# Value projection's first passes and their scaling placed ahead of the third chunk's u, and block 1's norm and transposes behind them

## The chip, the cores and the metric

The kernel runs on one NeuronCore of a Trainium2 chip. TensorE (PE) multiplies, VectorE (DVE), ScalarE (ACT) and GpSimd (POOL) do elementwise work, and SyncE (SP) issues most DMA transfers. The metric is the device time of one execution in microseconds; lower is better.

## The reference

The input is 8192 tokens (4 sequences of 2048) of 256 features, float32. One layer is computed, attention in chunks of 32 tokens and then a gated feed-forward network, each with a residual and a layer norm after it:

```python
Q, K, V = x @ W_q.T, x @ W_k.T, x @ W_v.T
mask[i, j] = decay ** (i - j) if i >= j else 0        # 32 x 32, decay = sigmoid(log_decay[0])
S = (Q K^T within each chunk) * mask
O = S V within each chunk
attn = (sigmoid(x @ W_g.T) * O) @ W_o.T + x
h = layernorm(x + attn)
u = silu(h @ wg.T) * (h @ wu.T)                       # 768 hidden features, int weights / 127
out = layernorm(h + u @ wd.T)
```

## The kernel before

**Tiling.** The tokens are cut into NB = 16 blocks of 512. Features lie on the 128 partitions where a matmul contracts over them (KD = 2 halves of 256), and tokens lie on the partitions where a norm runs over the features. The 768 hidden features are six chunks of 128, numbered hc = 0 to 5. PSUM has eight banks of 128 x 512 float32, one pool of which every product takes one in turn.

**Split products.** To keep float32 accuracy, a projection of the attention is three products. `token_parts` (L471 and on) splits the tokens x into x_hi (ScalarE, L479), x_lo (GpSimd, L480) and x_gap (VectorE, L486); the weights are split likewise. `three` (L533 and on) multiplies hi with hi and lo with lo into two PSUM banks (the first passes), has ScalarE scale each bank in place (L540), and returns a function that later adds the third product, gap with gap (the gap passes), and finishes. TensorE's gap passes need the scaled bank. `split_v` does so for the values v of a block (tile p_v, matmuls L521; its end, the v copies, on ScalarE at L572); `split_y`, `split_gate` and `split_out` do it for p_y, p_g (both L499) and p_o (L521).

**The feed-forward's chunks.** `ffn_up` (L822 and on) makes one hidden chunk: eight matmuls (L833) into the banks fg and fu; s = silu(fg) on ScalarE (L842); then, in its inner function `multiply`, u = fu * s on VectorE (L853), its cast u_hi on ScalarE (L858) and the remainder u_lo on GpSimd (L859). With `held=True` it returns `multiply` instead of calling it, so that other work can be put between s and u. `up_now` is `ffn_up` for one chunk, without holding. `ffn_down` (fdn, L704) contracts the six chunks' u_hi and u_lo.

**Norm and transposes.** `normalize` (L433) is four ScalarE instructions, one for each 128 tokens. `move_h` takes the normed h of a block: four 32 x 32 block transposes on VectorE into sq (L785), then 16 DMA transfers from SP into hT (L792). `split_h` casts hT to hT_hi on ScalarE (L809), and GpSimd makes hT_lo (L810); the next block's chunks multiply these.

**The loop.** Three blocks are in work at once. In pass b of the main loop (b = 0 to 13), the feed-forward of block b, the attention of block n = b + 2, the projections of block m = b + 3 and the loading of xT for block m + 1 are interleaved; m exists (`more`) for b = 0 to 12. Below, "block b" means pass b of this loop. Before block 0 stand the weights' preparation and the first blocks' attention; after block 13 the last two feed-forwards are finished.

**What sets the order.** Each engine works through its own queue. The order in it is the order in which the source lists the instructions, since most of them are recorded with `in_turn` or `in_steady_turn`, which fix it by hand; transfers from SP and some of GpSimd's work are placed by a scheduler. So the order of the calls in the loop is the order on TensorE, ScalarE and VectorE. The part of pass b that the change touches reads, before:

```python
        if b == 0:
            normalize(hs[b + 1], *scales_h)
            moving = move_h(b + 1, hs[b + 1])
        if m + 1 < NB:
            xTs[m + 1] = load_xT(m + 1)
        up_now(b, hT, uT, 2)
        if more:
            v_next, v_rest = split_v(m, x_parts)
            up_now(b, hT, uT, 3)
            v_rest()
```

In block 0 the norm of h_1 stands here, behind chunk 1; in every later block the norm of h_(b+1) stands ahead of chunk 0 and `move_h` behind chunk 1.

Of the kernel before, what the change touches and what calls it, by code (L numbers as in the profile page):

```python
# [76 lines left out]
def kernel(  # L77
# [20 lines left out]
    NB = NT // TB  # L98
# [29 lines left out]
    def load_xT(b, start=None, pieces=1):  # L128
        xt = xin.tile([P, KD, TB], F32, tag="xT", name=f"xT_{b}")
        src = xT[:, span(b, start)].rearrange("(k p) t -> p k t", p=P)  # L130
        n = KD // pieces
        for k in range(0, KD, n):
            queue(start).dma_start(xt[:, k : k + n, :], src[:, k : k + n, :])
        return xt
# [19 lines left out]
    xTs, xns = {}, {}  # L154
# [412 lines left out]
    def split_v(b, x_parts):  # L567
        v = work.tile([P, NG, D], F32, tag="v", name=f"v_{b}")
        per = TB // D

        def finish(i, pb):
            in_turn(nc.scalar.copy(flat(v, slice(i * per, (i + 1) * per)), pb))  # L572

        return v, three(f"v_{b}", token_major(w_parts["wv"], x_parts), finish)
# [68 lines left out]
    def attn_scores(b, yT):  # L643
        xt = xTs.pop(b)
        halves = [slice(i * PAIR, (i + 1) * PAIR) for i in range(P // PAIR)]
        ps = bank(f"ps_{b}")[:, : NG * PAIR].rearrange("p (g c) -> p g c", c=PAIR)
        for g in range(NG):
            for fc in range(KD):
                for rows in halves:
                    tokens = slice(g * P + rows.start, g * P + rows.stop)  # L650
                    product = nc.tensor.matmul(  # L651
                        ps[rows, g, :],
                        lhsT=xt[:, fc, tokens],
                        rhs=yT[:, fc, tokens],
                        start=(fc == 0),
                        stop=(fc == KD - 1),
                    )
                    in_turn(product)
        sTs.append(sTs.pop(0))
        sT = sTs[-1]  # L660
        for rows in halves:
            in_steady_turn(
                nc.vector.tensor_tensor(sT[rows, :, rows], ps[rows], mask[rows], ALU.mult)  # L663
            )
        return sT.rearrange("p g c -> p (g c)")
# [156 lines left out]
    def ffn_up(b, hT, uT, chunks, cols=slice(0, TB), held=False):  # L822

        n = cols.stop - cols.start
        for hc in chunks:
            pg = bank(f"fg_{b}_{hc}_{cols.start}")[:, :n]
            pu = bank(f"fu_{b}_{hc}_{cols.start}")[:, :n]

            kinds = (0, 1) if hc % 2 == 0 else (1, 0)
            for kind in kinds:  # L830
                for pb, w in ((pg, fg), (pu, fu)):
                    for dc in range(KD):
                        product = nc.tensor.matmul(  # L833
                            pb,
                            lhsT=w[kind][:, dc, hc * P : (hc + 1) * P],
                            rhs=hT[kind][:, dc, cols],
                            start=(kind == kinds[0] and dc == 0),
                            stop=(kind == kinds[1] and dc == KD - 1),
                        )
                        in_turn(product)  # L840
            s = work.tile([P, n], F32, tag="s", name=f"s_{b}_{hc}")
            in_turn(nc.scalar.activation(s, pg, AF.Silu, scale=SCALE / H_UP))  # L842
            no_more_splits()
            if len(uT[0]) == hc:
                for kind, dtype, tiles in zip(("hi", "lo"), (F32R, F16), uT):
                    tiles.append(
                        acts.tile([P, TB], dtype, tag=f"u_{kind}", name=f"u_{kind}_{b}_{hc}")
                    )

            def multiply(hc=hc, pu=pu, s=s):  # L850
                u = work.tile([P, n], F32, tag="u", name=f"u_{b}_{hc}")
                in_steady_turn(
                    nc.vector.scalar_tensor_tensor(u, pu, U_UP / H_UP, s, ALU.mult, ALU.mult)  # L853
                )
                hi, lo = uT[0][hc][:, cols], uT[1][hc][:, cols]

                def split():
                    in_steady_turn(nc.scalar.copy(hi, u))  # L858
                    nc.gpsimd.tensor_tensor(lo, u, hi.bitcast(F32), ALU.subtract)  # L859

                if lagging:
                    late_splits.append(split)
                else:
                    split()

            if held:
                return multiply
            multiply()
# [167 lines left out]
    def up_now(b, hT, uT, hc):  # L1036
        ffn_up(b, hT, uT, range(hc, hc + 1))

    for b in range(NB - 2):
        n = b + 2  # L1040
        m = b + 3
        more = m < NB
        xns[n] = load_xn(n)
        hT = hTs.pop(b)
        uT = [], []
        yT, v, sg = ahead
        if b:
            normalize(hs[b + 1], *scales_h)
        up_now(b, hT, uT, 0)
        if not more:  # L1050
            sT = attn_scores(n, yT)
        up_now(b, hT, uT, 1)
        if b:
            moving = move_h(b + 1, hs[b + 1])
        if more:
            sT = attn_scores(n, yT)
        if b == 0:
            normalize(hs[b + 1], *scales_h)
            moving = move_h(b + 1, hs[b + 1])
        if m + 1 < NB:  # L1060
            xTs[m + 1] = load_xT(m + 1)
        up_now(b, hT, uT, 2)
        if more:
            v_next, v_rest = split_v(m, x_parts)
            up_now(b, hT, uT, 3)
            v_rest()
            if scales_out is not None:
                normalize(r_before, *scales_out)
                store(b - 2, r_before)
        goT = attn_values(n, sT, v, sg)  # L1070
        if b == 0:
            look_up(range(4, n_pieces))
            cast_fd(0)
        if b == 1:
            count = count_wide()
            n_wide_early = const.tile([1, 1], I32, tag="n_wide_early", name="n_wide_early")
            nc.vector.tensor_copy(n_wide_early, count)
        go_parts, go_gaps = token_parts(goT, f"go_{n}")
        if more:
            y_next, y_rest = split_y(m, x_parts)  # L1080
        else:
            up_now(b, hT, uT, 3)
            normalize(r_before, *scales_out)
            store(b - 2, r_before)
        up_now(b, hT, uT, 4)
        go_gaps()
        up_now(b, hT, uT, 5)
        if b == 0:
            cast_fd(1)
        elif more:  # L1090
            hTs[b + 1] = split_h(b + 1, moving)
        r_before = r_out
        if more:
            y_rest()
            sg_next, g_rest = split_gate(m, x_parts)
            hs[n], out_rest = split_out(n, go_parts)
            g_rest()
            mv_h = out_rest()
            if b == 0:
                hTs[b + 1] = split_h(b + 1, moving)  # L1100
            ahead = y_next, v_next, sg_next
            if m + 1 < NB:
                x_parts, x_gaps = token_parts(xTs[m + 1], f"x_{m + 1}")
            std_h = root_in_turn(mv_h, of_h, f"h_{b}")
            if b:
                mv_before, std_before = mv_out, root_in_turn(mv_out, of_out, f"out_{b}")
            back_to_silu()

            def between():
                scales = scale_and_shift(mv_h, std_h, of_h, f"h_{b}")  # L1110
                if m + 1 < NB:
                    x_gaps()
                return scales

            r_out, mv_out, scales_h = ffn_down(b, uT, hs.pop(b), between)
            if b:
                scales_out = scale_and_shift(mv_before, std_before, of_out, f"out_{b}")
        else:
            hs[n], out_rest = split_out(n, go_parts)
            hTs[b + 1] = split_h(b + 1, moving)  # L1120
            scales_out = iterated_scale_and_shift(mv_out, of_out, f"out_{b}")
            normalize(r_before, *scales_out)
            store(b - 1, r_before)

            def amid():
                return iterated_scale_and_shift(out_rest(), (HALF, 1.0), f"h_{n}")

            r_out, mv_out, scales_h = ffn_down(
                b, uT, hs.pop(b), chunkwise=True, amid=amid
            )  # L1130
            normalize(hs[n], *scales_h)
            scales_out = iterated_scale_and_shift(mv_out, of_out, f"out_{b + 1}")
# [344 lines left out]
```

## Time and profile before

| | |
|---|---|
| median of 3 runs | 514.29 us (513.94 to 514.57) |
| the profiled execution's own time | 515.19 us |
| its span, first to last instruction | 513.6 us |
| TensorE matmul busy | 503.7 us, 98% of the span |
| ScalarE / VectorE / GpSimd busy | 73% / 60% / 57% |
| mean granted TensorE clock | 0.999 of full speed |

All times below are microseconds from the start of the span, unless they are durations. A row of the timeline has its start, its busy time, the engine, the source line, the operation with output <- inputs, and after an x how many like instructions it holds; in brackets may stand the idle time of the engine ahead of it and what ended that. A list of waits names the waiting engine and work, what it waited for, and then microseconds in total, the number of waits and the longest. PEld is TensorE's loading of weights, which overlaps matmuls.

### The profile page before, as it was taken

Reading aid. Unit: us, or ns where it says so; the run is one execution under the profiler, and the core shown is the slowest. Engines: PE = TensorE matmul, PEld = TensorE weight load, DVE = VectorE, ACT = ScalarE, POOL = GpSimd, SP = SyncE. Lnnn points to the kernel's source line nnn. Section 1 sums busy time; section 2 is a strip of 40 time slices with the busy share of each in tenths; the row PEclk is TensorE's granted clock in tenths of the full one; section 3 lists DMA queues with packets and bytes.
Section 4 is the critical chain, followed back from the end, with each engine's and each line's share of the span. In section 5 each row is a group of like instructions: output and inputs, shape, how many; then the busy total and the mean of one; then the engine's idle time right before and its main releaser. Section 6 shows DMA issues by size and latency. Waiting matters only on the chain.

```text
span 513.6 us, 9691 instructions
## 1 busy us (share of the span) xinstructions
PE 503.7 (98%) x3480; PEld 399.4 (78%) x3480; DVE 309.3 (60%) x725; ACT 373.1 (73%) x701; POOL 292.2 (57%) x324
## 2 busy tenths in 40 slices
PE   9999899999999999999999999999999999999995
PEld 5788677788878879787787878778787787877684
DVE  3977667564564647547474564647547464665654
ACT  4868686676868777686786868777686786766845
POOL 2835546554746557465464846557465564657764
PEclk9999999999999999999999999999999999999999
DMA  7720312112222122222212222122222211103112
GB/s 243 235 84 20 94 25 82 42 43 68 73 74 74 43 78 88 60 64 83 83 43 71 84 61 75 45 77 86 61 64 82 83 44 30 54 14 98 35 36 69
DMA packets 43315, 36.83 MB, mean 72 GB/s; under 512 B 4865, under 2 KB 39169, under 8 KB 43265
## 3 DMA queue, kind: packets, MB, share of 16 engines
q1 hardware_dynamic: 42144, 35.28, 22.9%
q10 hardware_dynamic: 1120, 0.92, 0.6%
q8 instruction: 28, 0.46, 0.4%
q14 instruction: 23, 0.18, 0.1%
HBM read 20.45 MB, written 8.39 MB: 56 GB/s over the span
## 4 chain that ended last, share of the span: by engine, by line
PE 74%; DVE 8%; ACT 7%; SPq 4%; issue 3%; POOL 2%; DMA 1%; DVEq 0%; ACTq 0%; POOLq 0%
PE fg L833 13%; PE fu L833 12%; PE fdn L704 11%; PE p_y L499 7%; PE p_g L499 7%; PE p_v L521 6%; PE p_o L521 6%; PE po L673 5%; SPq L792 4%; DVE u L853 3%; PE ps L651 2%; ACT s L842 2%; ACT h L433 1%; PE fdn L907 1%; DMA out_dram<-r 1%
## 5 line engine op out<-in xcount | busy, mean ns | idle before, releaser
L859 POOL TENSOR_TENSOR u_lo<-u,u_hi 128x512 f16<-128x512 f32 (+1 forms) x98 | 128.7, 1315 | 100.9 <-ACT u_hi L858 100.9
L853 DVE SCALAR_TENSOR_TENSOR u<-fu,s 128x512 f32<-128x512 f32 (+1 forms) x98 | 66.6, 680 | 127.1 <-ACT s L842 103.7
L858 ACT CAST u_hi<-u 128x512 fp32r<-128x512 f32 (+1 forms) x98 | 59.9, 612 | 85.0 <-DVE u L853 84.9
L833 PE MATMUL fg<-hT_hi,fg_hi 128*128 128x512 f32 (+1 forms) x196 | 71.1, 444 | 0.0
L842 ACT ACTIVATE s<-fg 128x512 f32<-128x512 f32 (+1 forms) x98 | 56.8, 580 | 6.3 <-PE fg L833 6.2
L833 PE MATMUL fu<-hT_hi,fu_hi 128*128 128x512 f32 (+1 forms) x196 | 60.6, 390 | 0.0
L833 PE MATMUL fg<-hT_lo,fg_lo 128*128 128x512 f16 (+1 forms) x196 | 58.2, 378 | 0.0
L833 PE MATMUL fu<-hT_lo,fu_lo 128*128 128x512 f16 (+1 forms) x196 | 57.4, 375 | 0.0
L480 POOL TENSOR_TENSOR go_lo<-goT,go_hi 128x512 fp32r<-128x512 f32 x30 | 38.7, 1313 | 26.3 <-ACT go_hi L479 26.3
L480 POOL TENSOR_TENSOR x_lo<-xT,x_hi 128x512 fp32r<-128x512 f32 x30 | 38.3, 1298 | 24.2 <-ACT x_hi L479 18.0
L744 DVE TENSOR_TENSOR h<-p_o,x 128x512 f32<-128x512 f32 x30 | 19.3, 686 | 42.5 <-PE p_o L521 32.4
L704 PE MATMUL fdn<-fd_hi,u_hi 128*128 128x256 f32 x312 | 44.7, 285 | 0.0
L833 PEld LDWEIGHTS fu<-hT_hi,fu_hi 128*128 128x128 f32 x196 | 36.5, 188 | 8.5
L833 PEld LDWEIGHTS fg<-hT_hi,fg_hi 128*128 128x128 f32 x196 | 34.7, 189 | 9.5
L704 PEld LDWEIGHTS fdn<-fd_hi,u_hi 128*128 128x128 f32 x312 | 39.0, 188 | 0.3
L433 ACT ACTIVATE h<-h,shift_h,scale_h 128x256 f32<-128x256 f32 x52 | 27.0, 590 | 16.8 <-POOL shift_h L396 16.8
L704 PE MATMUL fdn<-fd_lo,u_lo 128*128 128x256 f16 x312 | 38.6, 273 | 0.0
L810 POOL TENSOR_TENSOR hT_lo<-hT,hT_hi 128x512 f16<-128x512 f32 x28 | 35.5, 1290 | 3.7 <-ACT hT_hi L809 3.7
L833 PEld LDWEIGHTS <-fu_lo 128*128 128x128 f16 x196 | 19.2, 98 | 22.4 <-issue 0.3
L673 PE MATMUL po<-sT,v 128*128 128x128 f32 x256 | 31.2, 275 | 0.3 <-DVE sT L663 0.3
L704 PEld LDWEIGHTS <-u_lo 128*128 128x128 f16 x312 | 28.4, 98 | 3.9
L673 PEld LDWEIGHTS po<-sT,v 128*128 128x128 f32 x256 | 30.0, 192 | 0.7 <-PE p_v L521 0.5
(176 smaller groups left out, 1067.2 us busy)
## 6 DMA issues: line engine op xcount, KB each, us to landing
x<-in_x_dram SPq DMA_DIRECT2D x16, 512.0 KB, 3.5
xT<-in_xT_dram SPq DMA_DIRECT2D x15, 512.0 KB, 3.7
hT<-sq SPq DMA_DIRECT2D x224, 32.0 KB, 1.9
out_dram<-r SPq DMA_DIRECT2D x13, 512.0 KB, 3.1
out_dram<-r SPq DMA_DIRECT2D x7, 128.0 KB, 1.7
fg_int<-in_ffn_gT_dram SPq DMA_DIRECT2D x3, 256.0 KB, 7.0
fu_int<-in_ffn_uT_dram SPq DMA_DIRECT2D x3, 256.0 KB, 7.2
fd_int<-in_ffn_dT_dram SPq DMA_DIRECT2D x3, 256.0 KB, 5.9
```

The costliest lines, as they stand in the source:

```text
L433: nc.scalar.activation(r[:, g, :], r[:, g, :], AF.Identity, bias=shift[:, g : g + 1], scale=scale[:, g : g + 1],)
L480: in_turn(nc.gpsimd.tensor_tensor(lo[:, k, :], t[:, k, :], whole, ALU.subtract))
L499: nc.tensor.matmul(pb, lhsT=a[kind][:, k, i * P : (i + 1) * P], rhs=b[kind][:, k, :], start=kind + k == 0, stop=True, skip_group_check=True,)
L521: nc.tensor.matmul(pb[:, j * D : (j + 1) * D], lhsT=b[kind][:, k, g * P : (g + 1) * P], rhs=a[kind][:, k, :], start=kind + k + j == 0, sto ...
L673: product = nc.tensor.matmul(po[:, cols], lhsT=v[:, g, dc * P : (dc + 1) * P], rhs=sT[:, cols], start=True, stop=True,)
L704: product = nc.tensor.matmul(pb[:, j * D : (j + 1) * D], lhsT=part[:, g * P : (g + 1) * P], rhs=w, start=(i == 0), stop=(i == len(terms) - 1),
L810: nc.gpsimd.tensor_tensor(in_order[1], whole, in_order[0].bitcast(F32), ALU.subtract)
L833: product = nc.tensor.matmul(pb, lhsT=w[kind][:, dc, hc * P : (hc + 1) * P], rhs=hT[kind][:, dc, cols], start=(kind == kinds[0] and dc == ...
L842: in_turn(nc.scalar.activation(s, pg, AF.Silu, scale=SCALE / H_UP))
L853: nc.vector.scalar_tensor_tensor(u, pu, U_UP / H_UP, s, ALU.mult, ALU.mult)
L858: in_steady_turn(nc.scalar.copy(hi, u))
L859: nc.gpsimd.tensor_tensor(lo, u, hi.bitcast(F32), ALU.subtract)
```

## The change

The third chunk (hc = 2) is called with `held=True`, so its matmuls and s are issued, but not yet u. Then `split_v` issues the value projection's first passes and their two scalings, and only then `multiply` issues u, u_hi and u_lo of that chunk. In block 0 the norm of h_1 and `move_h` come after this instead of before the chunk. In block 13 there is no value projection, so the chunk is as it was. No instruction is added or taken out.

In the built program, TensorE's order is the same as before, and so is that of SP's transfers. On ScalarE, blocks 0 to 12 have s_2, p_v scaling, p_v scaling, u_hi_2, s_3 where they had s_2, u_hi_2, p_v scaling, p_v scaling, s_3; in block 0 the four norm instructions stand between u_hi_2 and s_3, where they stood ahead of s_2. On VectorE only block 0 differs: u_2 stands ahead of the four transposes instead of behind them. GpSimd's order is unchanged.

```diff
         if more:
             sT = attn_scores(n, yT)
+        if m + 1 < NB:
+            xTs[m + 1] = load_xT(m + 1)
+        multiply = ffn_up(b, hT, uT, range(2, 3), held=True)
+        if more:
+            v_next, v_rest = split_v(m, x_parts)
+        multiply()
         if b == 0:
             normalize(hs[b + 1], *scales_h)
             moving = move_h(b + 1, hs[b + 1])
-        if m + 1 < NB:
-            xTs[m + 1] = load_xT(m + 1)
-        up_now(b, hT, uT, 2)
         if more:
-            v_next, v_rest = split_v(m, x_parts)
             up_now(b, hT, uT, 3)
             v_rest()
             if scales_out is not None:
```

## The prediction

> **What bounds the kernel.** I read the page first: engine shares, then waits.
>
> ```profile
> PE 503.7 (98%) x3480; PEld 399.4 (78%) x3480; DVE 309.3 (60%) x725; ACT 373.1 (73%) x701; POOL 292.2 (57%) x324
> ```
>
> TensorE is the bound, so only its idle moments can be won or lost. The list of waits over the whole span has one large entry of TensorE on another engine:
>
> ```profile
> PEld p_v L521 <- ACT p_v L540: 6.4, 13, 2.0
> ...
> PE p_v L521 <- ACT p_v L540: 2.5, 3, 1.6
> ```
>
> 13 times, once in each of blocks b = 0 to 12, the gap passes of the value projection (wv_gap times x_gap) wait for ScalarE's scaling of p_v. The timeline shows why; block 0, rows of other work left out:
>
> ```profile
> 56.27 2.08 ACT L433 ACTIVATE h<-h,term_h,y_h 128x256 f32<-128x256 f32 x4
> ...
> 56.73 0.63 PE L521 MATMUL p_v<-wv_lo,x_lo 128*128 128x256 f32 x4
> ...
> 58.26 0.57 ACT L842 ACTIVATE s<-fg 128x512 f32<-128x512 f32 x1
> ...
> 58.55 0.63 PE L833 MATMUL fu<-hT_hi,fu_hi 128*128 128x512 f32 x2
> ...
> 59.64 0.62 ACT L858 CAST u_hi<-u 128x512 fp32r<-128x512 f32 x1 [0.81 <-DVE u L853]
> 60.16 1.06 ACT L540 ACTIVATE p_v<-p_v 128x512 f32<-128x512 f32 x2
> ...
> 60.80 1.22 PE L521 MATMUL p_v<-wv_gap,x_gap 128*128 128x256 f32 x8 [1.61 <-ACT p_v L540]
> 61.15 0.59 ACT L842 ACTIVATE s<-fg 128x512 f32<-128x512 f32 x1
> ```
>
> The first passes end at 57.36 (56.73 + 0.63), yet their scaling starts at 60.16: it stands in ScalarE's queue behind the norm of h_1, s_2, and the cast u_hi_2, which waits 0.81 for u_2. A later block has no norm there, but the same queue:
>
> ```profile
> 182.31 0.63 PE L521 MATMUL p_v<-wv_lo,x_lo 128*128 128x256 f32 x4
> ...
> 183.44 0.62 ACT L858 CAST u_hi<-u 128x512 fp32r<-128x512 f32 x1 [1.68 <-DVE u L853]
> ...
> 183.96 1.06 ACT L540 ACTIVATE p_v<-p_v 128x512 f32<-128x512 f32 x2
> ...
> 184.13 0.63 PE L833 MATMUL fu<-hT_hi,fu_hi 128*128 128x512 f32 x2
> ...
> 184.59 1.02 PEld L521 LDWEIGHTS p_v<-wv_gap,x_gap 128*128 128x128 f32 x8 [0.27 <-ACT p_v L540]
> 184.60 1.21 PE L521 MATMUL p_v<-wv_gap,x_gap 128*128 128x256 f32 x8
> ```
>
> Here the first gap pass is on time, but the row takes 1.21 where p_o's like takes 1.10: the second bank's scaling, done at 185.02, comes late.
>
> I measure each stall by starts. Rows of two 128x512 matmuls follow each other every 0.47 us; eight unstalled 128x256 gap passes take 0.94 (the chain's p_o pieces). So the stall is the start of the next matmul (po), less the start of the last fu row, less 0.47 and 0.94. Block 0: 61.85 - 58.55 - 1.41 = **1.89**. Block 1: **0.94**. Blocks 2 to 12: 0.08, 0.07, 0.11, 0.11, 0.10, 0.10, 0.08, 0.46, 0.08, 0.20, 0.11, together **1.50**. All: 4.33 us.
>
> **What the Trainium skill says.** "TensorE: Matmul & The Clock Gate", section "Architectural detail: the array is 16× 32×32, not 1× 128×128", says that ScalarE and VectorE work strictly first in, first out, while TensorE may only pull weight loads ahead. The trace agrees: ready scaling waits 2.8 us (57.36 to 60.16) behind a cast. "Perfetto Trace Analysis", section "Summary: the profiler window per engine type", says that waits lie outside an instruction's window and that TensorE's end is an estimate; so I use starts, and the trace's p_v rows (0.63 long, 0.47 apart) show the need. "DMA: Bandwidth & Descriptors", section "Anatomy of one DMA — SWDGE (gpsimd) path", gives about 2.0 us fixed per DMA, for GpSimd's path; the hT pieces here, from SP, show 1.8 / 1.9 / 3.6 (min, median, max).
>
> **The change, part by part.** No instruction is added or removed, and the built order of TensorE and of SP's transfers is the same. What moves:
>
> *Blocks 1 to 12, ScalarE.* Two scalings go ahead of u_hi_2. In block 4: s_2 ends 181.75; the first bank's passes end about 181.9, its scaling runs to 182.5; the second's end at 182.94 (182.31 + 0.63), scaling 183.0 to 183.6, over a second before TensorE asks at 184.60. u_hi_2 waited for u_2 until 183.44 anyway (VectorE's order is unchanged here), and now runs 183.55 to 184.15: 0.1 late. Behind it: POOL's u_lo_2 (0.1 late, needed only by u_4's buffer and by fdn, microseconds later) and s_3. s_3 stood behind the scalings at 184.95; now it waits only for its matmuls (183.48 + 0.82 = 184.30): ScalarE gains 0.6 up to the v copies. So each stall goes entirely: block 1's 0.94 and the 1.50. What is late next? The scaling of p_g: in block 3 it frees the bank about 0.2 before TensorE needs it. The 0.6 lead widens that. hT's cast, just ahead of it in ScalarE's queue, could start 0.6 earlier; in block 7 at 287.4 instead of 288.01, the last hT piece having been issued at 284.2 and landing 1.9 later, 286.1. Cost 0; if that cover failed, up to 0.1 a block would return.
>
> *Block 0, ScalarE.* The norm (four, 2.08) goes behind u_hi_2. By rows: s_2 56.27; scalings 56.80 and 57.40 (the second waits for TensorE's 57.36); u_2 on VectorE from 56.95; u_hi_2 57.9; norm 58.42; s_3 60.41 instead of 61.15. That is **0.74** earlier: the 0.81 wait for u_2 is filled. TensorE's stall of 1.89 goes, but ScalarE, 0.74 ahead, is what it meets next. From s_3 to p_o's scaling ScalarE runs without waiting for TensorE (the casts fd_hi and fd_lo are in there), and ends here:
>
> ```profile
> 73.06 1.06 ACT L540 ACTIVATE p_g<-p_g 128x512 f32<-128x512 f32 x2
> ...
> 73.78 1.13 PE L499 MATMUL p_g<-x_gap,wg_gap 128*128 128x512 f32 x4
> 74.05 1.05 ACT L540 ACTIVATE p_o<-p_o 128x512 f32<-128x512 f32 x2
> ```
>
> TensorE would arrive at 73.78 - 1.89 = 71.89; the first p_g bank is scaled at 72.88. It waits there, then for p_o's scalings, and leaves the block 0.74 earlier, not 1.89.
>
> *Block 0, VectorE and SP.* u_2 goes ahead of the four transposes, which follow the norm and end at about 60.98 instead of 58.83, just before s_3 ends and u_3 starts (61.0). hT_1's 16 DMAs (10.3 us of issue) start 2.15 later, and the last lands near 70.7 + 1.9 = 72.6 (74.3 with the longest landing). The cast hT_hi would run at 75.96 - 0.74 = 75.2. So nothing waits. SP's next transfer, x_4, starts at 76.82 when its buffer is free; xT_4 stays ahead of hT_1. PSUM banks: p1_y takes u_2's, fg_4 s_3's, fu_4 u_3's; these are done at 57.7, 61.0 and 61.8 and asked for at about 62.7, 63.6 and 64.1. POOL's u_lo_2 comes earlier.
>
> Sum: 0.74 + 0.94 + 1.50 = **3.18 us** on the profiled execution, 515.19 (span 513.6 and 1.59 around it): 512.0. It is 0.90 above the median of 514.29; of the stalls, block 9's 0.36 above its like and block 11's 0.10 look like chance of this execution. For the median I count 2.8: **511.5 us**.
>
> Costs the trace cannot show: whether VectorE and POOL disturb each other more when their overlaps shift. The nearest row is x_gap in block 0, 2.17 for two against 1.26 in block 1, which I read as one such clash at 0.9; off TensorE's path it costs nothing. I take 0, and -0.3 to +0.9. Block 6 lost about 0.3 at p_g, p_o; a 0.6 lead might save it: 0, bound -0.3.
>
> **Rivals.**
> - *Block 0 keeps all of its 1.89* (p_g not bound by ScalarE): 2.8 + 1.15 gives 510.3. For: other blocks' p_g has some cover. Against: the rows above, with ScalarE 0.2 from TensorE already.
> - *The wait moves on in every block* to p_g or p_o, and only part is won: blocks 0 and 1 alone give 1.68, 512.6; block 0 alone gives 513.55, within noise. For: ScalarE is busy 73% and its margin at p_g was 0.2. Against: the 0.6 it gains.
> - *Slower: hT_1 lands too late.* Place: ScalarE's queue ahead of x_hi, and POOL's chain to shift_h, on which block 1's norm already waited 1.8. Each microsecond past 75.2 delays block 1; about 1.0 is absorbed at block 1's p_v. To end 1.03 slower it must lose 2.8 + 1.03, so land after about 80; that needs a mean issue near 1.1 us instead of 0.6. One issue of 1.69 is the longest seen; were all like it, landing at 61 + 27 + 1.9 = 90 would cost some 13: 525. Against: the median issue is 0.595.
> - *Nothing changes*, because scheduling restores the old order: the built order excludes it.
>
> **How the numbers follow.** About 0.2%, 1.03 us, is what a measurement of this kernel can tell from no change. Forecast as worked: 0.70. All of block 0: 0.08. Only part: 0.15, of which 0.05 within 1.03. Slower: 0.05, and 0.02 for a small loss within it. So faster 0.88, same 0.07, slower 0.05. The range runs from 510.4 (3.18 with block 6's 0.3 and a little of block 0's rest) to 513.0 (block 1's or the later stalls half kept, a clash of 0.9 on the path).
>
> **What would show it.** In the trace after: the wait of p_v on the p_v scaling nearly gone (6.4 to under 1); eight p_v gap passes 0.94 before po in every block; in block 0, ScalarE in the order s_2, p_v, p_v, u_hi_2, norm, s_3 at 60.4, and a new stall of about 1 at p_g there; period of later blocks about 30.55 instead of 30.6 to 31.0. It is wrong if p_g or p_o gap passes of later blocks wait more than 0.1, if hT_hi waits for DMA, or if block 0 gains clearly other than 0.74.

## The result, and the profile after

The changed kernel takes a median of **510.81 us** (510.29 to 511.66, 4 runs) against 514.29 (513.94 to 514.57, 4 runs): ratio 0.9934, 95% interval 0.9917 to 0.9951. The gain is 3.48 us; the forecast was 511.5 (510.4 to 513.0), so the result lies inside the range, 0.7 below the time forecast. The profiled execution took 511.11, span 509.6, at a mean granted clock of 0.998. From the page of the changed kernel:

```profile
PE 501.2 (98%) x3480; PEld 400.3 (79%) x3480; DVE 309.3 (61%) x725; ACT 375.6 (74%) x701; POOL 291.8 (57%) x324
```

TensorE's busy time fell by 2.5 us with as many instructions, part of it in the gap rows of p_v, which take 1.10 where they took 1.21. Its waits on the other engines, in the two lists of waits (TensorE's matmuls, its weight loads):

```profile
PE p_g L499 <- ACT p_g L540: 0.9, 1, 0.9
...
PEld p_g L499 <- ACT p_g L540: 1.2, 2, 1.1
...
PEld p_o L521 <- ACT p_o L540: 0.2, 1, 0.2
```

The 13 waits of p_v on its scaling (6.4 us) are gone from both; one new stall stands at p_g. Block 0 in the timeline after (this execution reached block 0 0.56 sooner, so 0.56 is to be added when a start is compared with one before):

```profile
55.70 0.59 ACT L842 ACTIVATE s<-fg 128x512 f32<-128x512 f32 x1
...
56.19 1.23 ACT L540 ACTIVATE p_v<-p_v 128x512 f32<-128x512 f32 x2
...
57.33 0.61 ACT L858 CAST u_hi<-u 128x512 fp32r<-128x512 f32 x1
...
57.84 2.08 ACT L433 ACTIVATE h<-h,term_h,y_h 128x256 f32<-128x256 f32 x4
57.99 0.63 PE L833 MATMUL fu<-hT_hi,fu_hi 128*128 128x512 f32 x2
...
58.46 1.10 PE L521 MATMUL p_v<-wv_gap,x_gap 128*128 128x256 f32 x8
...
59.40 1.95 PE L673 MATMUL po<-sT,v 128*128 128x128 f32 x16
59.82 0.58 ACT L842 ACTIVATE s<-fg 128x512 f32<-128x512 f32 x1
...
71.73 1.05 ACT L540 ACTIVATE p_g<-p_g 128x512 f32<-128x512 f32 x2
72.36 0.30 PEld L499 LDWEIGHTS p_g<-x_gap,wg_gap 128*128 128x128 f32 x2 [1.06 <-ACT p_g L540]
72.36 1.21 PE L499 MATMUL p_g<-x_gap,wg_gap 128*128 128x512 f32 x4 [0.86 <-ACT p_g L540]
```

ScalarE runs s_2, two scalings, u_hi_2, norm, s_3 with no wait between, but for 0.13 within the row of scalings, where the second bank's first passes end. From the last fu row to po are 59.40 - 57.99 = 1.41 us, exactly a row of two (0.47) and eight gap passes (0.94): no stall at p_v. The 1.89 has become a stall at p_g and p_o. Block 4, answering to the rows shown before:

```profile
179.61 0.58 ACT L540 ACTIVATE p_v<-p_v 128x512 f32<-128x512 f32 x1 [0.28 <-PE p_v L521]
...
180.55 0.58 ACT L540 ACTIVATE p_v<-p_v 128x512 f32<-128x512 f32 x1 [0.36 <-PE p_v L521]
...
181.04 0.61 ACT L858 CAST u_hi<-u 128x512 fp32r<-128x512 f32 x1
...
181.70 0.63 PE L833 MATMUL fu<-hT_hi,fu_hi 128*128 128x512 f32 x2
...
181.96 0.60 ACT L842 ACTIVATE s<-fg 128x512 f32<-128x512 f32 x1 [0.30 <-PE fg L833]
182.17 1.10 PE L521 MATMUL p_v<-wv_gap,x_gap 128*128 128x256 f32 x8
...
183.11 1.05 PE L673 MATMUL po<-sT,v 128*128 128x128 f32 x8
```

ScalarE's waits are now on TensorE (0.28, 0.36, 0.30): it has caught up. In place of the 1.68 that it stood on u_2 it does the two scalings.

Where the time came from, by TensorE's starts (a block's period is from its first ps matmul to the next block's):

| us | before | after | gained |
|---|---|---|---|
| start of block 0 | 52.33 | 51.77 | 0.56 |
| block 0 | 32.54 | 31.74 | 0.80 |
| block 1 | 31.81 | 30.86 | 0.95 |
| blocks 2 to 12 | 336.08 | 334.29 | 1.79 |
| from block 13 to the end | 60.89 | 60.90 | -0.02 |
| span | 513.65 | 509.56 | 4.08 |

The first row isn't the change's: over all profiled executions here, whatever the kernel, block 0 starts between 50.97 and 52.41. So below I compare the **loop**, block 0 to 12: 400.43 before, 396.89 after, **3.54** less.

### The profile page after: what moved, and what is told of

Read it like the earlier page. It is cut to its first block, busy times and chain, and to the rows that moved or that the text cites. A ratio compares the mean times of both kernels' runs of the same rounds, so it can differ in the third digit from the quotient of the medians.

```text
span 509.6 us, 9690 instructions
## 1 busy us (share of the span) xinstructions
PE 501.2 (98%) x3480; PEld 400.3 (79%) x3480; DVE 309.3 (61%) x725; ACT 375.6 (74%) x701; POOL 291.8 (57%) x324
## 4 chain that ended last, share of the span: by engine, by line
PE 90%; DVE 4%; ACT 4%; issue 1%; POOL 1%; DVEq 0%; POOLq 0%; ACTq 0%
PE fg L833 16%; PE fu L833 15%; PE fdn L704 14%; PE p_v L521 8%; PE p_g L499 8%; PE p_y L499 8%; PE p_o L521 7%; PE po L673 5%; PE ps L651 3%; DVE u L853 1%; PE fdn L907 1%; ACT s L842 1%; PE pi L193 1%; PE pg L583 1%; PE pv L625 1%
## 5 line engine op out<-in xcount | busy, mean ns | idle before, releaser
L682 DVE SCALAR_TENSOR_TENSOR goT<-sg,po 128x512 f32<-128x512 f32 x32 | 21.9, 687 | 15.4 <-PE po L673 15.2
```

## The experiments

**The two halves of the change.** Changed kernel, the new order of calls only where a condition holds:

```diff
+        ahead_of_u = b == 0        # block0_only;  b > 0 in later_only
...
         multiply = ffn_up(b, hT, uT, range(2, 3), held=True)
+        if not ahead_of_u:
+            multiply()
         if more:
             v_next, v_rest = split_v(m, x_parts)
-        multiply()
+        if ahead_of_u:
+            multiply()
...
```

(with block 0's norm and transposes where the order needs them). The changed kernel itself ran beside them.

> The changed kernel unaltered, as the yardstick for the other kernels on this chip. My theory: TensorE's stall ahead of p_v's gap passes is gone in blocks 1 to 12 (2.7 us), block 0 is 0.8 shorter, sum 3.5 off the time before: about 510.8. Rival (some of the first difference was chance at the start of the span, which was 0.56 shorter in the changed kernel's profile): 511.3.

> Only block 0 has the new order (scalings ahead of u_hi_2, norm and transposes behind it); blocks 1 to 12 have the old one. My theory: block 0 gains what ScalarE gains, 0.8, and no more, since p_g's scaling is late there; blocks 1 to 12 stall as before (block 1: 0.94, the others 0.07 to 0.46). 0.8 off the time before, 513.5. Rival A, that block 0's move alone frees the later blocks too (an earlier block 0 leaves ScalarE ahead): 510.8. Rival B, that block 0 keeps its whole 1.89: 512.4.

> Only blocks 1 to 12 have the new order; block 0 has the old one. My theory: block 0 stalls 1.89 as before, all other p_v stalls are gone, period of blocks 2 to 12 is 30.55: 2.7 off the time before, 511.6. Rival, that the later blocks' gain rests on block 0's: close to the time before, 513.5 or more.

Measured, against 514.45 before on that chip: changed kernel 511.21 (ratio 0.9931, 0.9917 to 0.9944), block 0 alone 513.46 (0.9984, 0.9977 to 0.9992), later blocks alone 512.17 (0.9951, 0.9938 to 0.9965). The gains add: 0.99 + 2.28 = 3.27 against 3.24. The later half's 2.28 is short of the 2.7 expected, and the changed kernel is nearer to 511.3 than to 510.8; both hold the stretch ahead of block 0, which differs by up to 1.4 from one execution to another. By the loop alone the later half gains 2.74, and the changed kernel's loop takes 396.89 again. The rivals of the two halves are refuted. Within block 0, the move of the scalings and that of the norm were not tried apart. In the traces block 0's period is 31.74 with its own half and 32.54 without. With the later half all blocks from 2 to 11 take 30.55 or 30.56. With block 0's half alone they are as before, and block 6 takes 30.96 and block 9 31.01: to 0.01 us what they took in the trace before.

**Are those larger stalls chance?** The prediction had left 0.46 us out of the sum as "chance of this execution". The kernel before, once more:

> The kernel before, unchanged, for another profiled execution. If the larger stalls of blocks 6 (0.41 longer period), 9 (0.46) and 11 (0.2) were chance of one execution, as the prediction took them, they are elsewhere or absent now: periods of blocks 2 to 12 then all within 30.60 to 30.70. If they belong to the place in the program, the same blocks have them again: block 6 about 30.96, block 9 about 31.01, block 11 about 30.75, and behind them VectorE's u_4 of block 6 and second residual of block 8 about 0.33 late again.

One run, 513.93. Periods of blocks 6, 9, 11: 31.04, 31.02, 30.76 (in the first trace 30.96, 31.01, 30.76). So they are no chance. In each trace of this order VectorE starts u_4 of block 6 about 0.35 late against the other blocks, and the residual r behind the feed-forward (L887, "second residual" in the expectations; the first of its two instructions in the block) of block 8 some 0.3 late (0.24 in the first trace). u_4 in the trace of this run, by VectorE's timeline:

```profile
252.88 0.69 DVE L853 SCALAR_TENSOR_TENSOR u<-fu,s 128x512 f32<-128x512 f32 x1 [4.54 <-PE fg L833]
```

In the changed kernel both delays are still there (u_4 of block 6 at 251.00, 0.35 behind the other blocks'), and no period shows them.

**Do they belong to what those blocks do, or to where they stand in VectorE's instructions?** The kernel before with three, and with twenty, instructions at its start that write an unused tile:

```diff
     nc.vector.memset(eps, EPS)
+    pad = const.tile([P, 1], F32, tag="pad", name="pad")
+    for _ in range(3):             # 20 in pad20
+        nc.vector.memset(pad, 0.0)
```

> The kernel before with three further VectorE instructions at the very start (a 128x1 tile set to 0 three times, well before the first block; nothing reads it). No engine's order is otherwise changed. Theory (the recurring delays of about 0.35 us belong to positions in VectorE's stream of instructions, so three more instructions ahead move them onto others, as in the kernel with fd_lo on VectorE, which has three more too and shows none in blocks 6 and 8): the delays at u_4 of block 6 and at the second residual of block 8 are gone, and with them the extra 0.4 us of the periods of blocks 6 and 9, unless they now stand where they cost as much: up to 0.8 us faster than before, 513.6. Rival (they belong to what those blocks do, or to the time in the execution): still there, periods 30.96 and 31.01, time as before, 514.4.

> The same with twenty such instructions at the start. Theory (position in the stream): the delays stand some twenty VectorE instructions earlier in the work than before, so near the residuals and norm statistics at the end of block 5 and near yT in block 8, or are hidden there; blocks 6 and 9 lose their extra 0.4 unless they are hit again: between 513.6 and 514.4. Rival (place in the work or time): as before, periods 30.96 and 31.01.

With three: 513.84 against 514.47 (0.9985, 0.9977 to 0.9994). Blocks 6 and 9 take 30.62 and 30.63. u_4 of block 6 is on time, and u_1 of block 11 is late instead (lines are three higher in this kernel):

```profile
253.30 0.69 DVE L856 SCALAR_TENSOR_TENSOR u<-fu,s 128x512 f32<-128x512 f32 x1 [4.19 <-ACT s L845]
...
394.15 0.69 DVE L856 SCALAR_TENSOR_TENSOR u<-fu,s 128x512 f32<-128x512 f32 x1 [1.59 <-ACT s L845]
```

The idle time of 1.59 ahead of that u_1 is 1.24 without the three, and block 11 takes 30.98 instead of 30.76. With twenty: 514.19 (0.9997, 0.9988 to 1.0005), blocks 6 and 9 normal, blocks 8 and 11 at 30.93 and 31.00: the delays stand at u_4 of block 8 and at r of block 10. The theory holds: the delays follow the position in VectorE's stream. My guess of where twenty would put them was wrong but for the gain's bounds.

**How much room does ScalarE have now?** The changed kernel with one or two ScalarE instructions more in each of blocks 1 to 12:

```diff
             up_now(b, hT, uT, 3)
             v_rest()
+            if b:
+                for i in range(1):             # 2 in filler2
+                    part = flat(v_next, slice(2 * i, 2 * i + 2))
+                    in_turn(nc.scalar.mul(part, part, 1.0))
```

> The changed kernel with one further ScalarE instruction in each of blocks 1 to 12: half of v multiplied by 1.0 in place behind the v copies, so no value changes; about 0.53 us each, 6.4 us of ScalarE in all. Theory (the change gave ScalarE a lead of about 0.73 us at the p_g bank, and only the lead's end costs time): 0.73 - 0.53 leaves 0.2, so ten blocks keep their 30.55 and only blocks 6 and 9, whose recurring delay is 0.35, stall by about 0.15 each: 0.3 us over the changed kernel, about 511.5. Rival (any ScalarE work in the loop costs its time, the lead is not there): 6.4 us, about 517.5. Rival (the recurring delays were chance): no block stalls, 511.2.

> The changed kernel with two such instructions in each of blocks 1 to 12 (the other half of v too, by 1.0, no value changes): 1.06 us a block. Theory: 0.73 - 1.06 is -0.33, so each of the twelve blocks stalls about 0.33 at the p_g and p_o gap passes, or slightly less where another wait further on gives it back: up to 4.0 us, with 0.35 more in blocks 6 and 9: about 515.5. Rival (ScalarE is no limit at p_g): 511.2, no stall. Rival (all ScalarE work costs): 12.7 us, about 524.

Against 514.76 on that chip: 511.80 (0.9946, 0.9932 to 0.9959) and 518.53 (1.0078, 1.0063 to 1.0094). In the loop, one costs 0.85 over the changed kernel and two cost 6.43 (0.3 and 4.3 expected). So the lead is real, but I had it too large. Block 4, ScalarE's scaling of p_o and TensorE's gap passes on it, in the kernel before:

```profile
197.73 1.04 ACT L540 ACTIVATE p_o<-p_o 128x512 f32<-128x512 f32 x2
...
198.54 1.10 PE L521 MATMUL p_o<-wo_gap,go_gap 128*128 128x256 f32 x8
```

in the changed kernel:

```profile
194.76 1.08 ACT L540 ACTIVATE p_o<-p_o 128x512 f32<-128x512 f32 x2
...
195.98 1.10 PE L521 MATMUL p_o<-wo_gap,go_gap 128*128 128x256 f32 x8
```

and with one filler:

```profile
195.05 1.05 ACT L540 ACTIVATE p_o<-p_o 128x512 f32<-128x512 f32 x2
...
195.66 1.02 PEld L521 LDWEIGHTS p_o<-wo_gap,go_gap 128*128 128x128 f32 x8 [0.17 <-ACT p_o L540]
195.77 1.11 PE L521 MATMUL p_o<-wo_gap,go_gap 128*128 128x256 f32 x8
```

From the scaling's start to the gap passes are 0.81, 1.22 and 0.72; at 0.72 the weight load waits and the period is 0.04 longer. So p_o runs short before the 0.73 that I had put at p_g is used: measured from there, the lead at p_o is 0.50 at most, and before the change it was 0.09. One filler of 0.53 uses it up: block 6, whose u_4 is 0.35 late, then takes 31.01 where it took 30.55. The second is paid in full: periods of blocks 2 to 11 are 31.10 to 31.13 (31.44 in block 6), 0.55 more. Block 9 stays at 30.61 with one filler, as the delay of block 8 is spent where ScalarE waits for fg_3 anyway. Block 1 pays for neither (30.87): behind its v copies ScalarE waits for TensorE, in the changed kernel 0.41 at p_y and 0.74 at s_4, and the fillers fill these waits (with two, 0.22 is left at s_4, which starts at the same place in the block).

**The rest of block 0's stall.** Block 0's norm one step later, between s_3 and u_hi_3:

```diff
-            up_now(b, hT, uT, 3)
+            multiply = ffn_up(b, hT, uT, range(3, 4), held=True)
+            if b == 0:
+                normalize(hs[b + 1], *scales_h)
+            multiply()
+            if b == 0:
+                moving = move_h(b + 1, hs[b + 1])
```

(the norm and `move_h` taken from their place ahead of it);

> The changed kernel with block 0's norm and transposes one step further on: the norm of h_1 between s_3 and u_hi_3 on ScalarE, u_3 ahead of the transposes on VectorE. If block 0's remaining stall of 1.1 us is ScalarE's run from the norm to p_g, with its wait for fg_3's matmuls and for u_3 filled, ScalarE gains another 0.5 or so: block 0's period 31.2 instead of 31.74, total 510.7 against 511.2. If the stall at p_g has another cause (VectorE's fd, or x_gap), nothing: 511.2. If hT_1's transfers, now about 0.9 later, land too late for hT_hi, block 1 loses time: above 511.2.

or the casts fd_lo (three, 1.7 us of ScalarE, block 0, ahead of p_g's scaling) given to VectorE; and both:

```diff
-        def cast(kind):
+        def cast(kind, copy=nc.scalar.copy):
...
-            cast_fd(1)
+            cast_fd(1, nc.vector.tensor_copy)
```

> The changed kernel, with the three casts fd_lo of block 0 (1.65 us on ScalarE, just ahead of p_g's scaling) moved to VectorE, which is idle there. My theory, that ScalarE's queue is what took 1.1 of block 0's 1.89: p_g's scaling comes 1.6 earlier, TensorE's stall at p_g in block 0 (0.86 to 1.1) goes, and the time falls by 1.0 to 1.1 against the changed kernel: 509.7. Rival, that p_g's gap passes wait for something else (the p_g or p_o products' banks, go_lo): no change, 510.8. Rival, that VectorE becomes late with yT or the casts delay fdn: 510.8 or slower.

> The changed kernel with block 0's fd_lo casts on VectorE and its norm between s_3 and u_hi_3, both at once. Theory (with fd_lo on VectorE block 0 has no stall left, period 30.56): nothing more to gain, the time of fd_lo on VectorE alone, about 509.5. Rival (the later norm sends hT_1 about 0.9 later, and with ScalarE no longer late hT_hi now meets it): hT_hi waits up to about 0.5 for a transfer and block 0 or 1 loses some of it, 509.5 to 510.

> The kernel with fd_lo on VectorE once more, beside the two changes together on one chip: 509.4, block 0's period 30.56, and, if delays belong to positions in the stream, the 0.36 at u_1 of block 11 again and none in blocks 6 and 8.

The later norm: 510.35 against 514.76 (0.9913, 0.9900 to 0.9927), block 0's period 31.24, 0.50 less, as expected. fd_lo on VectorE: 509.34 against 514.45 (0.9902, 0.9886 to 0.9917), and 509.77 against 514.47 (0.9907, 0.9891 to 0.9922): block 0 takes 30.56 and 30.55, no stall is left. Both: 509.69 (0.9905, 0.9890 to 0.9920), period 30.55, the same. Block 0 with fd_lo on VectorE:

```profile
68.93 2.56 DVE L295 CAST fd_lo<-fd_int 128x512 f16<-128x512 int32 x3
...
69.58 1.06 ACT L540 ACTIVATE p_g<-p_g 128x512 f32<-128x512 f32 x2
...
70.76 1.09 PE L499 MATMUL p_g<-x_gap,wg_gap 128*128 128x512 f32 x4
...
72.47 1.16 ACT L809 CAST hT_hi<-hT 128x512 fp32r<-128x512 f32 x2
```

p_g's scaling starts 1.18 ahead of the gap passes instead of 0.63, and block 0's hT_hi, now 1.6 us earlier against the block's start, shows no wait for a transfer; nor does it with both, where the issue of the last hT_1 transfer ends at 71.73 and hT_hi starts at 73.06. So the stall that was left was ScalarE's run from the norm to p_g, nothing of VectorE's or SP's, and fd_lo on VectorE beats the changed kernel: 0.9902 and 0.9907 against 0.9931 and 0.9934.

## Why the prediction was right, and where it was short

*The mechanism* held: ready scalings stood in ScalarE's queue behind a cast that waited. This is the strict order of "TensorE: Matmul & The Clock Gate", section "Architectural detail: the array is 16× 32×32, not 1× 128×128", and the trace after agrees: scalings ahead, and every p_v stall is 0.00. One reading was loose: the 2.8 us of block 0 were not spent behind the cast alone, but behind the norm, s_2 and the cast, whose own wait was 0.81.

*Block 0*: predicted 0.74, measured 0.80. s_3 was to start at 60.41 and starts at 59.82 + 0.56 = 60.38. The stall at p_g and p_o was to be about 1.0; TensorE loses 1.02 ahead of p_g and some 0.17 within the gap passes, and moving fd_lo gives back 1.18.

*hT_1*: issue from 60.42 for 10.33 us, so done at 70.75 (71.31 on the old scale, 70.7 predicted); hT_hi at 74.63 (75.19, predicted 75.2), without a wait. The slower rival had nothing. But the prediction also named a hT_hi that waits for DMA as a sign of being wrong, and in later blocks it shows: before, no hT_hi of the loop waits; in the changed kernel block 1's waits 0.12 (0.29 in after_again, 0.47 in norm_in_s3), and in the first trace block 9's too:

```profile
345.81 1.14 ACT L809 CAST hT_hi<-hT 128x512 fp32r<-128x512 f32 x2 [0.22 <-DMA hT<-sq]
...
346.86 1.06 ACT L540 ACTIVATE p_g<-p_g 128x512 f32<-128x512 f32 x2
```

So the cover of hT's cast is used up in these places. The prediction had reckoned with up to 0.1 a block in that case. Nothing is lost: ScalarE's lead takes it up, and the periods of blocks 1 and 9 are 30.87 and 30.55 in all three runs.

*Blocks 1 to 12*: block 1 gave 0.95 for 0.94, blocks 2 to 12 gave 1.79 for 1.50. The 0.29 is chiefly block 6's stall of about 0.3 at p_g and p_o, which the prediction had seen and set to 0.

*The term that was mis-sized* is the discount from 3.18 on the profiled execution to 2.8 for the median, for "block 9's 0.36 above its like and block 11's 0.10" (which would give 2.72). With block 6's 0.3 and block 0's 0.06 it makes up the difference of the loop's 3.54 to 2.8. These stalls stand in both traces of the kernel before and in block0_only at the same instructions, so the median has them too. The 0.90 by which the profiled execution lay above the median came, as far as two traces tell, from ahead of block 0: before_again, 1.26 shorter in all, began block 0 1.36 earlier and took as long for the loop (400.50 against 400.43).

What the change does to these stalls is of two kinds; VectorE is as late as ever. In blocks 9 and 11 the late u_2 held up the p_v scalings through u_hi_2, and now they do not stand behind it. Block 9 before:

```profile
337.35 0.62 ACT L858 CAST u_hi<-u 128x512 fp32r<-128x512 f32 x1 [1.68 <-DVE u L853]
...
337.88 1.06 ACT L540 ACTIVATE p_v<-p_v 128x512 f32<-128x512 f32 x2
...
338.51 1.22 PE L521 MATMUL p_v<-wv_gap,x_gap 128*128 128x256 f32 x8 [0.18 <-ACT p_v L540]
```

and after, where u_hi_2 waits for u_2 and s_3 is still on time:

```profile
332.38 0.58 ACT L540 ACTIVATE p_v<-p_v 128x512 f32<-128x512 f32 x1
...
333.32 0.58 ACT L540 ACTIVATE p_v<-p_v 128x512 f32<-128x512 f32 x1 [0.36 <-PE p_v L521]
...
334.12 0.62 ACT L858 CAST u_hi<-u 128x512 fp32r<-128x512 f32 x1 [0.22 <-DVE u L853]
...
334.73 0.60 ACT L842 ACTIVATE s<-fg 128x512 f32<-128x512 f32 x1
...
334.94 1.10 PE L521 MATMUL p_v<-wv_gap,x_gap 128*128 128x256 f32 x8
```

In block 6, where the late u_4 comes behind all this, it is the lead: ScalarE, 0.50 ahead at p_o instead of 0.09, takes up 0.35 before TensorE sees it. filler1 tells the two apart: it takes the lead away, and block 6 pays 0.46, block 9 nearly nothing (30.61).

*The rival "the wait moves on in every block"* is refuted as the change stands: no p_g or p_o wait in later blocks. filler2 shows how near it was: with 1.06 us more on ScalarE, p_g's gap passes start 0.38 late in every block from 2 on (0.72 in block 6), and some 0.15 more is lost within them and p_o's.

## What to carry to other kernels

When a queue's head waits on another engine and work behind it is ready, put that work ahead; then follow the same queue to its next deadline: there the gain is the smaller of two amounts, the wait that was taken from the waiting engine and the time that the queue itself has gained (1.89 and 0.74 in block 0). Measure the slack at every consumer (p_o here, not p_g), and price it with a filler. A stall that sits at one block of many is to be looked for in a second trace before it is written off as chance.

## What was not expected of the hardware

The delays of VectorE. The page of before_again has instruction queues in its list of DMA queues (packets, MB, share of 16 engines):

```profile
q8 instruction: 28, 0.46, 0.4%
q14 instruction: 22, 0.18, 0.1%
```

The trace holds the time of each packet. Of q14's packets of 8192 bytes, one row moves when instructions are added to VectorE: at 107.66, 172.21, 253.55, 325.18 and 396.00 in the loop of before_again, at 93.83, 169.71, 234.13, 315.32 and 386.91 with twenty more; the others keep their place within 0.8. With three more, the packet at 253.55 comes at 247.58 and the one at 325.18 at 322.96. In every kernel where u_4 or r is late, such a packet starts 0.67 to 1.20 after that instruction (1.75 behind u_4 in filler2); behind the late u_1 of block 11 it is about 2.

"Runtime: NRT & Kernel Launch", section "Instruction fetch mechanics", says that a sequencer fetches its instructions through a DMA queue of its own, block by block while it works, and that crossing from a block to the next is mostly hidden. The trace agrees that instructions come by DMA queues while the engines work, but it names only two, and not all of q14's packets move with VectorE's instructions. It agrees on "mostly": of five such packets in the loop before, two go with a delay of about 0.35, u_4's in spite of 4.2 us in which VectorE had nothing to do, one with a delay of less than 0.1 (block 11) and two with none that I could see. That crossing a block is what delays the instruction fits all of this, but was not tried by itself, and why some crossings cost nothing stays open.
